# Adding layer 3 into a residual that is already stored: a four-layer network on one core

## The chip, the core and the metric

The kernel runs on one core of a Trainium2 chip. A core has a matrix engine (TensorE, PE in the profile; its weight loads are shown as PEld), a vector engine (VectorE, DVE), a scalar engine (ScalarE, ACT), a general engine (GpSimd, POOL) and a queue engine (SyncE, SP) that here only issues DMAs. Sixteen DMA engines move data between the large memory (HBM) and the on-chip memory (SBUF); PE writes its results into a small accumulation memory (PSUM) from which ACT and DVE take them. Each engine works through its own instruction list in order and waits on semaphores. The metric is the device time of one execution in microseconds, lower is better.

## What is computed

The input x has 16 images of 64 x 64 positions ("tokens", 4096 for each image) with 256 channels. Four layers follow one another, each with the same frame: normalise by groups of channels (`_gn`), compute something, add it to x.

```python
x = x + _L0_conv_ref(_gn(x), L0_conv_embeddings)   # nearest of 1024 code vectors
x = x + _L1_conv_ref(_gn(x), ...)                  # sigmoid attention along image rows
x = x + _L2_conv_ref(_gn(x), ...)                  # gate * _gn(x), gate from an n x n softmax
x = x + _L3_conv_ref(_gn(x), ...)                  # linear attention, output projection, layer norm
return x
```

Of layer 3 the end matters here:

```python
out = jnp.einsum('bhde,bhdn->bhen', context, q)
...
out = jnp.einsum('bxyh,hc->bxyc', out, w_out) + b_out
mu = jnp.mean(out, axis=-1, keepdims=True)
var = jnp.mean(jnp.square(out - mu), axis=-1, keepdims=True)
out = (out - mu) * jax.lax.rsqrt(var + LN_EPS) * gamma + beta
```

All arithmetic is in float32.

## The kernel before

**Stages.** Each image goes through a sequence of Python generators: `stats0` (statistics of x), `stage1` (layer 0, the search for the nearest code), `layer1`, `rows2` and `stage2` (layer 2's exponentials), `gate2` (applies the gate), `stage3` (layer 3). The main loop at the end of the function gives each generator a start time and a length in units of one image's period, puts them in a heap, and always advances the generator whose next step is due first. So the instruction lists of all engines interleave the stages of up to five images, and the order is fixed when the program is built; `LAG` and `LEN` constants set the shifts. In the steady state a period is some 340 us long. Toward the end there are fewer images left to interleave; the last image's layer 3 runs nearly alone.

**Chunks.** An image is worked on in 8 chunks (`NCHUNK`) of 512 tokens (`CW`). Most tiles hold a chunk as 128 partitions by 2 halves (`NK`) of the channels by 512 tokens, that is, channels on the partitions, 512 KB. Chunks go from one stage to the next through HBM: `dram.tile` gives such an array, with a few buffers for each name.

**gate2** (from line 663) loads a chunk of layer 2's input, multiplies it by the gate so that it becomes the input of layer 3, takes statistics (`chunk_stats`), and stores it into the HBM tile `d` (line 691, SP's queue; the profile names it `x_g<-xg_g`). It leaves off an amount that is constant for each channel: `xm_` (line 670), beta minus the mean of layer 2's normalisation, is handed on to `stage3` to be added there.

**stage3, first part** (lines 740 to 796) loads each chunk of that array (line 742, `xk_s<-x_g`), and makes keys, queries and values and the context matrix. The tile `qv` has tag `u4`, two buffers. In its first chunk it also makes `x_row` (line 771): `put_row` turns `xm_` into a row in three bf16 parts, with eight filler matmuls (`busy`, line 133) before it. Queries are stored to HBM and fetched again in the second part (`fetch`, `qo_s<-qd_s`).

**stage3, second part** (lines 797 to 908) is what the change touches. `form`, `variance` and `deviate` run one or two chunks ahead and scale the queries by the layer norm's factor; `variance` ends in a power on GpSimd (line 850). For each chunk the loop at line 872 loads the residual again (line 874, `xo_s<-x_g`), and forms each output bank `px` in PSUM, twice per chunk, from three products: the residual transposed to tokens on partitions (line 884, eight 128 x 128 transposes per chunk), the scaled queries times `wctx` (line 890), and ones times `x_row` (line 894). ACT copies the bank into `y` (line 895), which has tokens on its partitions and tag `u4` too. SP stores y one chunk later (line 905; the last at 908) in the order of the output, rows of 1 KB.

**GpSimd's list.** GpSimd's own DMAs are those of the search: for each tile of 128 tokens an indirect DMA gathers the code vectors from HBM and adds them to the tokens `xc` in SBUF (line 399). Between them stand small operations of all stages: the powers of lines 280 and 850, the queries' maximum and sum (784 and 738). Tokens with codes added are transposed by PE two tiles into the next chunk (`back`, line 362). The input of a chunk of tokens, and all other large loads, are on SP's queue.

## Time and profile before

Three runs took 5756.55, 5736.58 and 5745.39 us, median 5745.39. The profile is of one execution with its own span.

| | us | share of the span |
|---|---|---|
| span, first to last instruction | 5743.5 | |
| out phases of the last four images (first to last eviction of y) | 63, 59, 40, 36 | |
| search's last gather issued at | 5057.6 | |
| TensorE clock granted, mean | | 0.953 of full |
| DMA traffic, mean | | 184 GB/s |

The rest of the profile's lines stand in the prediction. How to read them: "busy" is the time in which an engine executes instructions (several matmuls that overlap count once), "idle before" is the time that the engine stood still just before such an instruction, and what ended that time is its releaser. The chain of waits goes back from the last instruction, at each step to what released it. A row of groups names line, engine, operation, tile written from tiles read, and shape.

### The profile page before, as it was taken

The page shows a single profiled execution, that of the slowest core. Times are in us where ns is not written, and L with a number is a line of the kernel's source. Part 1 is how long each engine was busy: PE and PEld are TensorE (multiplying, and loading weights), DVE is VectorE, ACT ScalarE, POOL GpSimd, SP SyncE. Part 2 cuts the span into 40 slices and gives each one's busy share as a digit, 9 for nine tenths or more (in the row PEclk, how much of TensorE's full clock was granted, in tenths as well). Part 3 has the DMA queues.
Part 4 walks back from the last instruction along what each step waited for, and adds up shares of the span by engine and source line. Part 5 has one row for each costly group of instructions (what it writes and reads, how often), then busy time and mean ns, then how long its engine had stood idle before and what let it go on. Part 6 is the DMA issues. An engine that isn't in the chain of part 4 may idle for free.

```text
span 5743.5 us, 80122 instructions
## 1 busy us (share of the span) xinstructions
PE 5264.6 (92%) x28975; PEld 3227.5 (56%) x28975; DVE 5074.3 (88%) x7186; ACT 4498.8 (78%) x6514; POOL 1721.5 (30%) x1074
## 2 busy tenths in 40 slices
PE   8978899889999999999999999999999999997888
PEld 3534455545656556565655656565565655664556
DVE  6489799999989999998999999999999999998882
ACT  4478588878878788887978788787888879887873
POOL 3123233223333232322323232332323233311221
PEclk9988999989999999999999999999999999998888
DMA  6453836655665656566475656746566674745543
GB/s 184 133 165 93 263 111 196 198 156 170 212 192 174 228 157 217 168 201 223 149 248 158 216 181 198 233 149 223 174 210 194 188 229 151 227 157 180 198 159 116
DMA packets 521380, 1059.52 MB, mean 184 GB/s; under 512 B 52504, under 2 KB 266392, under 8 KB 512792
## 3 DMA queue, kind: packets, MB, share of 16 engines
q1 hardware_dynamic: 406288, 885.11, 45.5%
q0 software_dynamic: 73728, 67.14, 8.2%
q10 hardware_dynamic: 40968, 102.13, 4.6%
q8 instruction: 230, 3.77, 0.3%
q14 instruction: 166, 1.36, 0.1%
HBM read 751.18 MB, written 303.04 MB: 184 GB/s over the span
## 4 chain that ended last, share of the span: by engine, by line
PE 40%; DVE 16%; ACT 11%; issue 4%; DMA 4%; POOL 4%; SPq 0%; ACTq 0%; POOLq 0%; DVEq 0%
PE pd_s L387 12%; DVE ex_s L630 6%; ACT ex_s L627 5%; PE ph_l L477 3%; PE pxo_s L890 3%; PE pqv_s L764 2%; PE pk_s L747 2%; PE po_l L515 2%; DMA qo_s<-qd_s 2%; PE pxo_s L884 2%; PE pz_s L839 2%; POOL qv_s L784 2%; DVE i_s L398 2%; DVE nn_s L393 1%; PE pvr_s L847 1%
## 5 line engine op out<-in xcount | busy, mean ns | idle before, releaser
L630 DVE CUSTOM_DVE_ANT_0 ex_s<-ex_s,x2b 128x2048 f32<-128x2048 f32 x1024 | 2398.0, 2349 | 65.9 <-ACT ex_s L627 65.8
L627 ACT ACTIVATE ex_s<-x0b,nmax_s,x_r 128x2048 f32<-128x2048 f32 x1024 | 2138.1, 2089 | 42.9 <-DVE num_s L630 34.3
L387 PE MATMUL pd_s<-e,xn_s 128*128 128x512 f32 x4096 | 1989.0, 620 | 44.9 <-DVE m L393 33.6
L399 POOL DMA_INDIRECT xc_s<-in_emb_rows,i_s x512 | 1091.3, 2131 | 1926.7 <-DVE i_s L398 1406.6
L387 PEld LDWEIGHTS pd_s<-e,xn_s 128*128 128x128 f32 x4096 | 752.8, 196 | 810.3 <-issue 697.6
L393 DVE CUSTOM_DVE_ANT_0 nn_s<-pd_s,nn_s 128x1024 f32<-128x1024 f32 x512 | 620.2, 1213 | 157.9 <-PE pd_s L387 87.4
L398 DVE FIND_INDEX8 i_s<-m,nn_s 128x8 uint32<-128x1024 f32 x512 | 623.4, 1218 | 0.0
L382 ACT ACTIVATE nn_s<-ne,nx_s 128x1024 f32<-128x1024 f32 x512 | 582.6, 1144 | 45.2 <-DVE nx_s L353 21.5
L477 PE MATMUL ph_l<-wh_l,xt_l 128*128 128x256 f32 x2048 | 525.5, 393 | 20.8 <-DVE m L393 12.1
L764 PE MATMUL pqv_s<-wqv_s,xk_s 128*128 128x256 f32 x2048 | 488.9, 380 | 0.0
L477 PEld LDWEIGHTS ph_l<-wh_l,xt_l 128*128 128x128 f32 x2048 | 382.3, 194 | 135.9 <-issue 64.1
L764 PEld LDWEIGHTS pqv_s<-wqv_s,xk_s 128*128 128x128 f32 x2048 | 388.8, 191 | 119.9 <-issue 60.2
L784 POOL TENSOR_TENSOR qv_s<-qv_s,qm_s 128x512 f32<-128x512 f32 x128 | 195.3, 1526 | 679.9 <-DVE qm_s L783 492.7
L850 POOL TENSOR_TENSOR lrs_s<-lrs_s,mhalf 128x4 f32<-128x4 f32 x128 | 163.6, 1278 | 678.0 <-ACT lrs_s L849 664.2
L515 PEld LDWEIGHTS po_l<-at_l,h_l 64*128 64x128 f32 x4096 | 260.6, 193 | 61.3 <-issue 29.1
L515 PE MATMUL po_l<-at_l,h_l 64*128 64x64 f32 x4096 | 288.7, 283 | 4.5 <-DVE m L393 2.9
L738 POOL TENSOR_TENSOR qv_s<-qv_s,qd_s 128x512 f32<-128x512 f32 x128 | 203.6, 1590 | 266.5 <-DVE qd_s L737 101.4
L890 PE MATMUL pxo_s<-wctx_s,qo_s 128*128 128x256 f32 x1024 | 272.8, 390 | 0.8 <-DVE qo_s L858 0.8
L895 ACT COPY y_s<-pxo_s 128x512 f32<-128x512 f32 x256 | 149.0, 582 | 153.7 <-PE pxo_s L894 131.7
L747 PE MATMUL pk_s<-xk_s,wk_s 128*128 128x512 f32 x512 | 256.6, 624 | 1.5 <-DMA xk_s<-x_g 1.5
L362 PE MATMUL pt_s<-ident,xc_s 128*128 128x128 f32 x1024 | 161.1, 287 | 101.5 <-DMA xc_s<-in_emb_rows,i_s 71.7
L332 ACT ACTIVATE xn_s<-xt_s,nb_n,s_n 128x512 f32<-128x512 f32 x256 | 200.9, 807 | 50.5 <-PE pd_s L387 28.4
(201 smaller groups left out, 7306.4 us busy)
## 6 DMA issues: line engine op xcount, KB each, us to landing
xs_s<-in_xT SPq DMA_DIRECT2D x128, 512.0 KB
xt_s<-in_xT SPq DMA_DIRECT2D x128, 512.0 KB
xc_s<-in_x SPq DMA_DIRECT2D x128, 512.0 KB
x_s<-xt_s ACTq DMA_DIRECT2D x128, 512.0 KB
xt_l<-x_s SPq DMA_DIRECT2D x128, 512.0 KB
x_l<-xt_l SPq DMA_DIRECT2D x128, 512.0 KB
xr_r<-x_l SPq DMA_DIRECT2D x128, 512.0 KB
xg_g<-x_l SPq DMA_DIRECT2D x128, 512.0 KB
```

The costliest lines, as they stand in the source:

```text
L382: nc.scalar.activation(nn, ne2, AF.Identity, bias=nx2[ch][:, t : t + 1])
L387: nc.tensor.matmul(pd[:, cols], lhsT=xn[ch][:, k, t * P : (t + 1) * P], rhs=e2[:, k, cols], start=(k == 0), stop=(k == NK - 1),)
L393: nc.vector.tensor_tensor_reduce(out=nn, in0=pd, in1=nn, scale=1.0, scalar=-3.0e38, op0=ALU.add, op1=ALU.max, accum_out=m8[:, 0:1],)
L398: nc.vector.max_index(i8, m8, nn)
L399: nc.gpsimd.indirect_dma_start(out=xc[ch][:, t, :], out_offset=None, in_=emb_rows, in_offset=bass.IndirectOffsetOnAxis(ap=i8[:, 0:1], axis=0),
L477: nc.tensor.matmul(ph[:, t, :], lhsT=X[:, k, t * P : (t + 1) * P], rhs=wh_n[:, k, :], start=(t % 2 == 0 and k == 0), stop=False, skip_grou ...
L515: nc.tensor.matmul(po[:, r, k * CH + t, :], lhsT=h[rows, t, k * P : (k + 1) * P], rhs=at[rows, t, :], start=True, stop=True,)
L627: nc.scalar.activation(ex, x0b, AF.Exp, bias=nmax[:, T : T + 1], scale=x01[:, T, 1:2], accum_out=den[:, h, T : T + 1])
L630: nc.vector.tensor_tensor_reduce(out=ex, in0=ex, in1=x2b, scale=1.0, scalar=0.0, op0=ALU.mult, op1=ALU.add, accum_out=num[:, h, T : T + 1],)
L747: nc.tensor.matmul(pk, lhsT=wk_n[:, k, :], rhs=xt[:, k, :], start=(k == 0), stop=(k == NK - 1))
L764: nc.tensor.matmul(pqv[:, j, :], lhsT=xt[:, k, t * P : (t + 1) * P], rhs=wqv_n[:, k, :], start=(j == 0 and k == 0), stop=False, skip_group ...
L890: nc.tensor.matmul(px[:, j, :], lhsT=qT[:, t * P : (t + 1) * P], rhs=wctx[:, 1, :], start=False, stop=False, skip_group_check=True,)
```

## The change

`gate2` stores the layer's input into the output array itself, and `stage3` computes only what layer 3 adds, with channels on the partitions, and has it added there by a DMA. Part by part:

- The HBM tile for the gated chunk is gone. `gate2` stores into `out[b]`, whose shape becomes 8 chunks x 128 partitions x 1024 (2 halves x 512 tokens), 4 KB in one run for each partition; the host puts the result back in the order of tokens afterwards. `stage3` loads its first part's chunks from there.
- `x_row`, `by_identity` and the eight fillers are gone. `xm_` is added when y is evicted: `nc.scalar.copy` becomes an activation (Identity) with `xm_` as a bias for each partition.
- The second load of the residual and its transposes are gone. The product with `wctx` is turned round: `wctx` is the stationary operand, one 128 x 128 block for each half of the channels, and the 512 scaled queries stream past it; two such matmuls for each chunk in place of four over 256 columns and two over the row.
- y has channels on its partitions, and is written to `out` by a DMA on GpSimd's queue with `accum_op=ALU.add`, in the same chunk, issued after `variance(ch + 2)`; SP's stores of y are gone.
- `qv` and `y`, which share tag `u4`, ask for three buffers in place of two (4 KB per partition each). SBUF set aside for the rings of descriptors of GpSimd's DMAs shrinks from 16384 bytes (the default) to 4096 bytes per partition.

```diff
--- before.py
+++ after.py
@@ -135,7 +135,7 @@
                 skip_group_check=True,
             )
 
-    h_row, qv_row, x_row = row_tile("h_row"), row_tile("qv_row"), row_tile("x_row")
+    h_row, qv_row = row_tile("h_row"), row_tile("qv_row")
 
     def twice(row):
         return row.unsqueeze(1).to_broadcast([P, 2, C])
@@ -168,13 +168,6 @@
                     skip_group_check=True,
                 )
         return make
-
-    def by_identity(out, v3, plus):
-        for k in range(NK):
-            nc.tensor.matmul(
-                out[:, k * P : (k + 1) * P], lhsT=v3[:, k, :], rhs=ident, start=(k == 0), stop=(k == NK - 1),
-                skip_group_check=True,
-            )
 
 
     e_raw = s2p.tile([P, NK, CODES], F32, tag="x0b", name="e_raw", bufs=2)
@@ -658,7 +651,7 @@
             yield from rest
 
 
-    x3_d, norm3 = {}, {}
+    norm3 = {}
 
     def gate2(b):
         tag = f"g2_{b}"
@@ -668,7 +661,7 @@
 
         xm_ = small.tile([P, NK], F32, tag="xm", name=f"xm_{tag}")
         nc.gpsimd.tensor_tensor(xm_, bet, nmean, ALU.subtract)
-        x3 = []
+        dst = out[b].rearrange("c p (k n) -> c p k n", k=NK)
 
         for ch in range(NCHUNK):
             xt = xg.tile([P, NK, CW], F32, tag="xg", name=f"xg_{tag}_{ch}")
@@ -687,19 +680,16 @@
                 )
             chunk_stats(st3, xt, ch)
             yield 4
-            d = dram.tile([P, NK, CW], F32, tag=f"x3_{ch}", name=f"x3_{tag}_{ch}", bufs=3)
-            nc.sync.dma_start(out=d, in_=xt)
-            x3.append(d)
+            nc.sync.dma_start(out=dst[ch], in_=xt)
         with tc.high_priority(offset=URGENT):
             scale, nmean, _ = gn_finish(st3, "n3", b)
-        x3_d[b], norm3[b] = x3, (scale, nmean, xm_)
+        norm3[b] = scale, nmean, xm_
         yield 2
 
 
     def stage3(b):
         tag = f"s3_{b}"
-        dst = out[b].rearrange("(t p) c -> p t c", p=P)
-        x3 = x3_d.pop(b)
+        x3 = out[b].rearrange("c p (k n) -> c p k n", k=NK)
         scale, nmean, xm_ = norm3.pop(b)
         wk_n = wts.tile([P, NK, P], F32, tag="wk_n", name=f"wk_{tag}")
         nc.sync.dma_start(out=wk_n, in_=w_src[:, :, 1, :])
@@ -754,7 +744,7 @@
                 nc.scalar.activation(al[:, ch : ch + 1], last, AF.Exp, scale=-1.0, bias=now)
             kx = s3p.tile([P, CW], F32, tag="v2", name=f"kx_{tag}_{ch}", bufs=7)
             nc.scalar.activation(kx, pk, AF.Exp, bias=now, accum_out=ks[:, ch : ch + 1])
-            qv = s3p.tile([P, CH, 2, P], F32, tag="u4", name=f"qv_{tag}_{ch}")
+            qv = s3p.tile([P, CH, 2, P], F32, tag="u4", name=f"qv_{tag}_{ch}", bufs=3)
             qvs[ch] = qv
             for pr in range(CH // 2):
                 pqv = bank(f"pqv_{tag}_{ch}_{pr}").rearrange("p (j n) -> p j n", j=2)
@@ -767,8 +757,6 @@
                         )
                 nc.tensor.matmul(pqv, lhsT=ones3, rhs=twice(qv_row), start=False, stop=True, skip_group_check=True)
                 nc.scalar.copy(qv[:, 2 * pr : 2 * pr + 2, :, :].rearrange("p j s n -> p j (s n)"), pqv)
-            if ch == 0:
-                put_row(x_row, xm_, by_identity, f"x_{tag}", idle=8)
             yield 5
             pkt = bank(f"pkt_{tag}_{ch}")
             for t in range(CH):
@@ -868,31 +856,15 @@
         deviate(0)
         variance(1)
         yield 2
-        before = None
         for ch in range(NCHUNK):
-            xt = xb.tile([P, NK, CW], F32, tag="xb", name=f"xo_{tag}_{ch}")
-            nc.sync.dma_start(out=xt, in_=x3[ch])
             qT = qs[ch]
-            y = s3p.tile([P, CH, C], F32, tag="u4", name=f"y_{tag}_{ch}")
-            for pr in range(2):
+            y = s3p.tile([P, NK, CW], F32, tag="u4", name=f"y_{tag}_{ch}", bufs=3)
+            for pr in range(NK):
                 if pr == 1 and ch + 1 < NCHUNK:
                     deviate(ch + 1)
-                px = bank(f"pxo_{tag}_{ch}_{pr}").rearrange("p (j c) -> p j c", c=C)
-                for j in range(2):
-                    t = 2 * pr + j
-                    for k in range(NK):
-                        nc.tensor.matmul(
-                            px[:, j, k * P : (k + 1) * P], lhsT=xt[:, k, t * P : (t + 1) * P], rhs=ident,
-                            is_transpose=True, start=(j == 0 and k == 0), stop=False, skip_group_check=True,
-                        )
-                for j in range(2):
-                    t = 2 * pr + j
-                    nc.tensor.matmul(
-                        px[:, j, :], lhsT=qT[:, t * P : (t + 1) * P], rhs=wctx[:, 1, :], start=False, stop=False,
-                        skip_group_check=True,
-                    )
-                nc.tensor.matmul(px, lhsT=ones3, rhs=twice(x_row), start=False, stop=True, skip_group_check=True)
-                nc.scalar.copy(y[:, 2 * pr : 2 * pr + 2, :], px)
+                px = bank(f"pxo_{tag}_{ch}_{pr}")
+                nc.tensor.matmul(px, lhsT=wctx[:, 1, pr * P : (pr + 1) * P], rhs=qT, start=True, stop=True)
+                nc.scalar.activation(y[:, pr, :], px, AF.Identity, bias=xm_[:, pr : pr + 1])
                 if pr == 0:
                     if ch + 2 < NCHUNK:
                         form(ch + 2)
@@ -901,11 +873,8 @@
                 else:
                     if ch + 2 < NCHUNK:
                         variance(ch + 2)
-                    if before is not None:
-                        nc.sync.dma_start(out=dst[:, (ch - 1) * CH : ch * CH, :], in_=before)
+                    nc.gpsimd.dma_start(out=x3[ch], in_=y, accum_op=ALU.add)
                 yield 3
-            before = y
-        nc.sync.dma_start(out=dst[:, TOK // P - CH :, :], in_=before)
 
 
 
@@ -967,14 +936,15 @@
         ("w_qkv", L3_conv_w_qkv), ("w_out", L3_conv_w_out), ("b_out", L3_conv_b_out),
         ("gamma", L3_conv_gamma), ("beta", L3_conv_beta),
     ]
-    nc = bacc.Bacc("TRN2", target_bir_lowering=False, num_devices=1)
+    nc = bacc.Bacc("TRN2", target_bir_lowering=False, num_devices=1, dynamic_dma_scratch_size=4096)
     arrays, args = {}, []
     for name, a in given:
         a = np.ascontiguousarray(a)
         arrays[f"in_{name}"] = a
         args.append(nc.dram_tensor(f"in_{name}", a.shape, mybir.dt.from_np(a.dtype), kind="ExternalInput").ap())
-    o = nc.dram_tensor("out_0", (x.shape[0], TOK, C), F32, kind="ExternalOutput").ap()
+    o = nc.dram_tensor("out_0", (x.shape[0], NCHUNK, P, NK * CW), F32, kind="ExternalOutput").ap()
     with tile.TileContext(nc) as tc:
         tile_net_kernel(tc, *args, o)
     r = run_bass_kernel_spmd(nc, [arrays], core_ids=[0])
-    return r.results[0]["out_0"].reshape(x.shape)
+    y = r.results[0]["out_0"].reshape(x.shape[0], NCHUNK, P, NK, CW)
+    return y.transpose(0, 1, 4, 3, 2).reshape(x.shape)
```

## The prediction

> **What bounds the kernel now.** I read the busy shares first, then the chain that ended last, then busy time by stretch, then what VectorE (DVE) waits for.
>
> ```profile
> span 5743.5 us, 80122 instructions
> PE 5264.6 (92%) x28975; PEld 3227.5 (56%) x28975; DVE 5074.3 (88%) x7186; ACT 4498.8 (78%) x6514; POOL 1721.5 (30%) x1074
> ...
> q1 hardware_dynamic: 406288, 885.11, 45.5%
> q0 software_dynamic: 73728, 67.14, 8.2%
> ...
> PE 40%; DVE 16%; ACT 11%; issue 4%; DMA 4%; POOL 4%; SPq 0%; ACTq 0%; POOLq 0%; DVEq 0%
> ```
>
> TensorE (PE) is at 92%, VectorE close behind; PE has the largest share of the chain. GpSimd (POOL) is idle for 70%. The next view splits the span into stretches: the first two are the same part of a batch period in different batches, 2874 to 2969 is one steady period's last part of layer 3 (the eight chunks that form y; "out phase" below), the last two are the out phases of the last two batches, where little else runs. Columns: length, busy PE, PEld, DVE, ACT, POOL, then granted clock, DMA share, GB/s.
>
> ```profile
> 1600.00:1851.00 251.00, 235.26 (x1197) 137.72 (x1196) 229.53 (x330) 205.43 (x300) 86.62 (x50) 0.94 0.55 171
> 2634.00:2874.00 240.00, 223.40 (x1204) 132.17 (x1203) 226.02 (x324) 204.89 (x300) 80.95 (x50) 0.99 0.57 179
> 2874.00:2969.00 95.00, 92.72 (x603) 62.88 (x601) 89.47 (x120) 74.41 (x107) 25.48 (x16) 1.00 0.76 242
> 5559.00:5599.00 40.00, 36.54 (x221) 28.52 (x219) 30.29 (x40) 24.62 (x39) 9.04 (x6) 0.99 0.74 248
> 5703.00:5743.00 40.00, 35.63 (x223) 28.86 (x221) 7.83 (x12) 10.97 (x22) 6.04 (x6) 1.00 0.58 185
> ```
>
> In a steady out phase PE is busy 92.7 of 95 us, but DVE is busy 89.5: PE is the first limit and DVE stands 3 us behind it. In the last out phase PE alone is full. The first two rows show how PE work turns into time: at clock 0.94 instead of 0.99 PE is busy 12 us longer, and the stretch is 11 us longer.
>
> **What is removed from PE.** These are the rows of groups, busy time in all and mean of one:
>
> ```profile
> L884 PE MATMUL pxo_s<-ident,xo_s 128*128 128x128 f32 x1024 | 166.5, 284 | 0.0
> L894 PE MATMUL pxo_s<-x_row,ones 128*128 128x512 bf16 x256 | 98.3, 384 | 0.0
> L133 PE MATMUL prow_x_s<-ones 128*128 128x512 bf16 x128 | 30.2, 379 | 0.0
> L174 PE MATMUL prow_x_s<-ident,v_x_s 128*3 128x128 f32 x64 | 10.0, 281 | 4.3 <-ACT v_x_s L146 4.3
> L155 PE MATMUL prow_x_s<-top_x_s,below 3*3 3x256 bf16 x32 | 8.7, 272 | 3.4 <-ACT top_x_s L154 3.4
> ```
>
> The transposes of the residual (L884), the row products (L894) and the whole making of x_row (fillers L133, L174, L155) go: 166.5 + 98.3 + 30.2 + 10.0 + 8.7 = 313.7 us of PE busy time, 19.6 us for each of 16 batches. The product with wctx stays, turned round: before 512 instructions over 256 columns (L890, 1024 records, 272.8 us), after 256 over 512 columns. The nearest row of that shape, L747, has 512 records in 256.6 us, and 512 records are what the new form gives. So 0 to -16 us; I take 0.
>
> **How much of that reaches the end: the steady part, 1500 to 5059 us.** It holds 10.4 periods of about 340 us. Two ceilings: PE loses 19.6 x 10.4 = 204 us there, and VectorE has only 3559.0 - 3314.7 = 244 us idle. What DVE waited for in this stretch (us in total, times, longest):
>
> ```profile
> DVE ex_s L630 <- ACT ex_s L627: 54.3, 48, 2.9
> DVE nn_s L393 <- ACT nn_s L382: 33.6, 31, 3.9
> DVE qz_s L841 <- PE pz_s L839: 19.4, 17, 4.2
> DVE nkm_s L750 <- PE pk_s L747: 17.7, 26, 1.9
> ```
>
> All lines of this view that name PE add up to 89 us, those that name ACT to 129. I take it that with PE 6% lighter the waits on PE go and those on ACT stay: **-89 us**, 8.6 per period. Bounds: 0 (DVE finds another wait) and -134, the chain's pieces in this stretch on L884 (73), L894 (32) and x_row's matmuls (29).
>
> **The clock's share.** Lighter PE work has a price: the first two stretches above show the clock lower and the period 11 us longer where PE pauses more often. Bounds per period: 0 and +11. I take 2, near the clean end, because the work leaves the out phase, the densest one (clock 1.00): **+22 us** over 10.4 periods. The Trainium skill ("TensorE: Matmul & The Clock Gate", What's actually happening) says that the clock falls to half after one idle window of some 3.4 us; by that rule, which speaks against thinning PE, one such window more in each period would be an estimated 1.7 us of lost matmul time, so about +18 us, which agrees with what I took and proves it no more than the rows do.
>
> **Head and tail.** Before 1500 us there is one out phase: -8, as for one period. In the tail the last two out phases take 40 us for eight chunks, about 5.2 us per chunk in the timeline. Per chunk two halves lose 0.46 (L884) + 0.22 (L894) us of chain each, 1.36 us; but the accumulating transfer then wants 3.7 us per chunk (below) and qo's load, 262 KB at 0.047, 0.8, so I take 4.2 instead of 5.2: -8 us each, **-16**. In the two out phases before these, the chain has 16.5 us on L884 and L894 and DVE is busy beside them; half, **-8**.
>
> **The accumulating DMA.** One per chunk, 128 in all, 512 KB each, from GpSimd's queue. No such DMA is in the trace; the nearest is L399, the codebook gather, which adds into its target as well:
>
> ```profile
> L399 POOL DMA_INDIRECT xc_s<-in_emb_rows,i_s x512: 1533/1602/3897, 42.3 to 5057.6; - x171
> ...
> DMA to landing us min/median/max: 3.6/5.6/12.2
> ```
>
> Issuing costs GpSimd 1.6 to 3.9 us; at L399's mean of 2.13 us it is 273 us more on an engine that is idle for 4022. DMA time: the queue table gives q0 8.2% of 16 x 5743.5 us for 67.14 MB, 0.112 us per KB, and q1 0.047. Bounds for 524 KB on 16 engines: 1.6 us as a plain copy, 3.7 us at the gather's rate; I take 3.7, since that row adds too. Removed are the reload of the residual and the plain store of y, 67 MB each at 0.047: 396 us of all 16 engines, against 470 added; the DMA share rises by some 1%, hidden at shares of 0.6 to 0.76.
>
> Order on GpSimd: the new DMA stands behind the power of chunk ch+2 (L850), which waits for an ACT instruction issued after y's eviction, so y is ready when GpSimd gets there. Its other waits (gate store landed, xk read) ended tens of us before. Behind it wait the next gather and the next L850. A gather may thus leave 2.1 us later and queue up to 3.7 behind on the same DMA queue. The fourth gather of a chunk issued at 2894.92 is read by the transposes (L362) from 2910.78, the one at 2944.02 from 2958.29: with 5.6 us to land, 10.3 and 8.7 us of cover against 5.8. So 0; without cover it would be up to 5.8 us at each of some 30 chunk ends, +174.
>
> The Trainium skill speaks against this queue: "SBUF — State Buffer", SBUF: two separate sides, says that GpSimd cannot write descriptors while DVE holds a shared port in some modes. L399's spread, 1.6 to 3.9, agrees that something holds it at times; by the rule each issue could be late by one long DVE instruction, an estimated 2.3 us more, 8.1 against the 8.7 of cover: the sum stays.
>
> Buffers: y shares tag u4 with qv. Three instead of two let y wait for its landing over three chunks: in the tail 12.6 us, against 2.7 (second half and its eviction) + 1.0 (L850) + 5.6 + 2.8 (landing, larger transfer) = 12.1. Tight, but it holds; if not, ACT stands at the eviction and all later ACT work with it. The smaller descriptor ring makes room for this buffer; with landings of 8 us and issues 4 us apart two or three DMAs are open at a time, and I take no wait for the ring: 0.
>
> End: the last plain store is issued at 5739.3 and the span ends 4.2 us later; the new one takes 5.6 + 2.8: **+4**. ACT's eviction changes from a copy (582 ns) to one with a bias (L579, same shape, 683): 256 x 0.10 = +27 us, less 20 for x_row's three ACT groups, beside an ACT that idles 22%: 0. SP loses 128 loads and its 128 waits for y; gate's store and xk's load stay, on another array: 0, at best a few us.
>
> Sum: -89 + 22 - 8 - 16 - 8 + 4 = -95, so a span of 5648; the median of the runs shown is 1.9 us above the profiled span: **5650 us**.
>
> **Rivals.** (1) *The clock takes it all*: every period pays the whole 11 us, 114 in place of 22: -3, 5742 us. For it: PE's clock in the head is 0.88 to 0.96 wherever PE is below 90%. Against: the out phase has it at 1.00. (2) *PE was the only limit*: the chain's pieces vanish whole, 134 + 8 + 39 (tail) - 4 = 177: 5568 us. For it: the 11 us for 12 of the two stretches. Against: DVE's 89.5 of 95. (3) *Slower: the accumulating transfer is slow.* Place: the tail's out phases, where chunks take 4.6 to 8 us and y's buffers hang on it. If one takes T, the last four out phases last 32 T instead of 63 + 59 + 40 + 36 = 198 us; outside them the gain is 89 + 8 - 22 - 4 = 71, so it decides from T = (198 + 71)/32 = 8.4 us, 2.3 times the gather's rate. At T = 11.9, one steady chunk, the loss is 32 x 11.9 - 198 - 71 = 112: 5857 us; beyond that the steady part slows too. Against it: the gather's rate; for it: no row shows an addition into HBM, and HBM must be read and written. (4) *It doesn't do what it says*: a wait between store, load and addition on the one output array, wider than its chunk, would hold SP; its price is rival 3's, and I count it there.
>
> **How the numbers follow.** Forecast 0.53, own range 5595 to 5715 (steady term between 45 and 134, tail 0 to 32). Rival 1: 0.12. Rival 2: 0.13. Rivals 3 and 4: 0.22. The range goes from just below rival 2, 5550, to 5800 (T near 10), which leaves out under 2 in 10. A change under 0.3%, 17 us, can't be told from none here: faster 0.66, same 0.12, slower 0.22.
>
> **What would show it.** After: PE busy near 4950 us and near 86 to 88% of the span; DVE above 89%; steady out phases of 90 to 92 us with PE near 77; the clock no lower than 0.94; one new POOL DMA line x128 of about 2 us, landing within 9 us; y's ACT row without waits on a DMA; last two out phases near 32 us. A landing over 12 us, ACT waiting for y's buffer, or SP waiting for that DMA would make it wrong on the slow side; a DVE share under 88% with waits on ACT or POOL would say that PE was not what DVE waited for.

## The result, and the profile after

The changed kernel took 5767.53 us (median of 5 runs, 5758.93 to 5774.41) against 5745.39 for the kernel before: ratio 1.0041, 95% interval 1.0021 to 1.0061. It is slightly slower, by 22 us, where 95 us less were forecast; the time lies inside the range, on the wrong side of the start. The profiled execution has a span of 5757.2 us. First the page of the changed kernel: busy shares, the two large DMA queues, the chain that ended last.

```profile
span 5757.2 us, 75894 instructions
PE 5151.4 (89%) x26959; PEld 3026.3 (53%) x26959; DVE 5053.7 (88%) x7186; ACT 4509.0 (78%) x6450; POOL 1880.5 (33%) x1201
...
q1 hardware_dynamic: 320272, 750.88, 39.1%
q0 software_dynamic: 92160, 134.26, 15.3%
...
PE 31%; DVE 21%; ACT 12%; issue 7%; DMA 4%; POOL 4%; ACTq 0%; SPq 0%; POOLq 0%; DVEq 0%
```

The work did leave: 2016 matmul records fewer, the transposes and row products among them. But PE's busy time fell by 113 us (5264.6 to 5151.4), not by the 314 that these rows had held. Rows of groups overlap: those of all PE groups add up to 5924 us before and 5702 after. PE lost 9 points of the chain and DVE won 5. By stretches (length; busy PE, PEld, DVE, ACT, POOL; granted clock, DMA share, GB/s): the rest of a steady period, its out phase, and the last out phases of the last two batches:

```profile
2609.00:2856.00 247.00, 226.59 (x1175) 133.20 (x1174) 223.16 (x326) 204.50 (x297) 84.29 (x53) 0.96 0.57 172
2856.00:2950.00 94.00, 88.20 (x513) 51.95 (x513) 90.22 (x120) 76.30 (x107) 33.71 (x22) 0.96 0.77 206
5583.00:5622.00 39.00, 29.92 (x120) 16.11 (x118) 27.73 (x38) 23.96 (x37) 13.99 (x13) 0.95 0.73 137
5717.00:5757.00 40.00, 27.72 (x118) 15.09 (x116) 8.90 (x13) 12.35 (x22) 13.72 (x14) 0.92 0.75 131
```

The thinned out phase is 1 us shorter (94 after 95). PE is busy 88.2 us there instead of the 77 forecast, at a clock of 0.96 instead of 1.00; DVE needs 90.2. The rest of the period, which lost only x_row's making (3 us by its rows), is 247 us instead of 240. So the later batches run at 342 us where they took 337. Ten whole periods, from the first eviction of y in the second batch to that in the twelfth, first in the kernel before, then in the changed one (columns as above):

```profile
1506.00:4888.00 3382.00, 3209.14 (x18088) 1979.22 (x18086) 3147.77 (x4439) 2799.03 (x4056) 1078.85 (x660) 0.98 0.62 195
1501.00:4912.00 3411.00, 3161.64 (x16841) 1866.63 (x16840) 3131.08 (x4444) 2806.83 (x4018) 1202.71 (x740) 0.95 0.62 181
```

The ten periods took 29 us more, with 47 us less of TensorE and as much of VectorE and ScalarE as before, within 17 us. The last stretch, which nothing but this chain fills, has PE busy 8 us less and is 40 us as before: its chunks are 3 us faster together, the landing at the end is 4 us longer. The groups of the new output path (busy, mean ns | idle before, releaser):

```profile
L838 POOL TENSOR_TENSOR lrs_s<-lrs_s,mhalf 128x4 f32<-128x4 f32 x128 | 195.1, 1524 | 154.4 <-ACT lrs_s L837 146.9 <-issue 7.3
L876 POOL DMA_DIRECT2D out<-y_s x128 | 122.0, 953 | 452.0 <-ACT lrs_s L837 224.2 <-ACT y_s L867 219.6 <-issue 3.5
L867 ACT ACTIVATE y_s<-pxo_s,xm_g 128x512 f32<-128x512 f32 x256 | 174.6, 683 | 108.6 <-PE pxo_s L866 105.7 <-issue 1.3 <-ACT xt_s L358 1.2
```

The adding DMA (L876) is cheap to issue, 0.95 us against the 2.13 assumed, and y's eviction (L867) waits for no DMA, so three buffers suffice. Its landing, in the view of this line:

```profile
DMA to landing us min/median/max: 5.4/6.5/8.5
```

That is inside the 9 us asked for. What DVE, and then PE, waited for in 1500 to 5059 us (total, times, longest):

```profile
DVE ex_s L623 <- ACT ex_s L620: 72.8, 38, 3.9
DVE qd_s L726 <- ACT qv_s L773: 46.2, 12, 6.5
DVE qz_s L829 <- PE pz_s L827: 33.5, 24, 5.2
DVE nn_s L386 <- ACT nn_s L375: 25.9, 23, 3.9
DVE nn_s L386 <- PE pd_s L380: 25.6, 22, 2.1
DVE nkm_s L740 <- PE pk_s L737: 19.7, 26, 1.8
```

```profile
PE ph_l L470 <- DVE xt_l L513: 40.8, 27, 3.9
PE pd_s L380 <- DVE m L386: 36.2, 30, 2.3
PE px_s L334 <- ACT sq_s L328: 29.3, 32, 2.7
```

This is the turn of the case. All DVE lines that name PE add up to 113 us where 89 were to vanish; those on ACT rose from 129 to 152. And PE, lighter, now waits for DVE: 125 us in this stretch, 38 before.

### The profile page after: what moved, and what is told of

It reads as the page before. It is cut to its first block, busy times and chain, and to the rows that moved or that the text cites. A ratio compares the mean times of both kernels' runs of the same rounds, so it can differ in the third digit from the quotient of the medians.

```text
span 5757.2 us, 75894 instructions
## 1 busy us (share of the span) xinstructions
PE 5151.4 (89%) x26959; PEld 3026.3 (53%) x26959; DVE 5053.7 (88%) x7186; ACT 4509.0 (78%) x6450; POOL 1880.5 (33%) x1201
## 3 DMA queue, kind: packets, MB, share of 16 engines
q0 software_dynamic: 92160, 134.26, 15.3%
## 4 chain that ended last, share of the span: by engine, by line
PE 31%; DVE 21%; ACT 12%; issue 7%; DMA 4%; POOL 4%; ACTq 0%; SPq 0%; POOLq 0%; DVEq 0%
PE pd_s L380 11%; DVE ex_s L623 8%; ACT ex_s L620 5%; PE ph_l L470 3%; DVE i_s L391 3%; PE pxo_s L866 2%; PE pk_s L737 2%; POOL qv_s L772 2%; DVE nn_s L386 2%; PE pqv_s L754 2%; DVE st_s L251 1%; PE po_l L508 1%; ACT nn_s L375 1%; DMA x0b<-rows_r 1%; PE pz_s L827 1%
## 5 line engine op out<-in xcount | busy, mean ns | idle before, releaser
L623 DVE CUSTOM_DVE_ANT_0 ex_s<-ex_s,x2b 128x2048 f32<-128x2048 f32 x1024 | 2372.6, 2322 | 89.1 <-ACT ex_s L620 88.5
L380 PE MATMUL pd_s<-e,xn_s 128*128 128x512 f32 x4096 | 2039.3, 635 | 71.3 <-DVE m L386 63.0
L392 POOL DMA_INDIRECT xc_s<-in_emb_rows,i_s x512 | 1122.0, 2191 | 1900.9 <-DVE i_s L391 1309.6
L380 PEld LDWEIGHTS pd_s<-e,xn_s 128*128 128x128 f32 x4096 | 775.4, 202 | 889.2 <-issue 743.4
L470 PE MATMUL ph_l<-wh_l,xt_l 128*128 128x256 f32 x2048 | 539.9, 401 | 62.0 <-DVE xt_l L513 40.8
L866 PE MATMUL pxo_s<-qo_s,wctx_s 128*128 128x512 f32 x512 | 286.1, 644 | 15.9 <-DVE qo_s L846 14.3
L728 POOL TENSOR_TENSOR qv_s<-qv_s,qd_s 128x512 f32<-128x512 f32 x128 | 177.9, 1390 | 320.7 <-DVE qd_s L727 204.4
L876 POOL DMA_DIRECT2D out<-y_s x128 | 122.0, 953 | 452.0 <-ACT lrs_s L837 224.2
L867 ACT ACTIVATE y_s<-pxo_s,xm_g 128x512 f32<-128x512 f32 x256 | 174.6, 683 | 108.6 <-PE pxo_s L866 105.7
L838 POOL TENSOR_TENSOR lrs_s<-lrs_s,mhalf 128x4 f32<-128x4 f32 x128 | 195.1, 1524 | 154.4 <-ACT lrs_s L837 146.9
```

The costliest lines, as they stand in the source:

```text
L380: nc.tensor.matmul(pd[:, cols], lhsT=xn[ch][:, k, t * P : (t + 1) * P], rhs=e2[:, k, cols], start=(k == 0), stop=(k == NK - 1),)
L392: nc.gpsimd.indirect_dma_start(out=xc[ch][:, t, :], out_offset=None, in_=emb_rows, in_offset=bass.IndirectOffsetOnAxis(ap=i8[:, 0:1], axis=0),
L470: nc.tensor.matmul(ph[:, t, :], lhsT=X[:, k, t * P : (t + 1) * P], rhs=wh_n[:, k, :], start=(t % 2 == 0 and k == 0), stop=False, skip_grou ...
L623: nc.vector.tensor_tensor_reduce(out=ex, in0=ex, in1=x2b, scale=1.0, scalar=0.0, op0=ALU.mult, op1=ALU.add, accum_out=num[:, h, T : T + 1],)
L866: nc.tensor.matmul(px, lhsT=wctx[:, 1, pr * P : (pr + 1) * P], rhs=qT, start=True, stop=True)
```

## The experiments

Each kernel was timed in five rounds beside the kernel before (5738 to 5742 us in these groups). Ratios are to that kernel, with 95% intervals.

**1. Is it the clock?** If PE, thinned, only lost its clock, discarded matmuls that fill the gaps should win time back. One kernel puts them into the out phase, one at the head of layer 3 where x_row's making had stood.

```diff
                 px = bank(f"pxo_{tag}_{ch}_{pr}")
+                busy(px, 3)
```

> The changed kernel with three filler matmuls (128x512 bf16, 0.22 us of chain each, as in x_row's fillers) before each of the 256 output banks of the second part of layer 3; nothing else differs. That puts back some 169 us of PE time where 265 were removed. Clock theory (the thinner PE list lets the granted clock fall more often, 222 us at half clock between 2874 and 5059 us against 58 before the change, and that costs what was saved): clock up from 0.934 to 0.945 or more, time down from 5767 by 10 to 60 us although PE has more to do. GpSimd theory (the accumulating DMA stands in front of the power of line 838 and holds the layer norm's chain): no gain, 5760 to 5800 us. If PE time simply adds: up to 5850.

Measured: 5818.15 us, 1.0129 (1.0103 to 1.0154), 50 us more than the changed kernel, at a granted clock of 0.942. The ranges of the clock theory and of the GpSimd theory are both missed; only the loose bound of adding PE time holds.

```diff
+            if ch == 0:
+                busy(bank(f"pfl_{tag}"), 8)
```

> The changed kernel with the eight filler matmuls put back in the first chunk of layer 3's first part, where the making of x_row had them, 1.8 us of PE chain per image. Clock theory: if the clock is lost there, 5 to 30 us less than 5767 and clock above 0.934; if it is lost in the thinned second part, no change within 10 us. GpSimd theory: no change, or some us more.

Measured: 5762.94 us, 1.0041 (1.0026 to 1.0057): as without. Filling gains nothing on balance. These runs can't tell a lost clock that costs nothing from one whose return is eaten by the fillers' own work.

**2. Is it the place of the DMA on GpSimd?** The addition is issued half a chunk later.

```diff
+                    if before is not None:
+                        nc.gpsimd.dma_start(out=x3[ch - 1], in_=before, accum_op=ALU.add)
...
-                    nc.gpsimd.dma_start(out=x3[ch], in_=y, accum_op=ALU.add)
```

> The changed kernel with each accumulating DMA issued half a chunk later, after the first eviction of the next chunk, so that GpSimd reaches the power of line 838 without waiting for y. GpSimd theory: GpSimd's waits at the DMA (444 us for y and the lrs eviction) shrink, waits of PE at line 845 (22.7 us) return to some 6 us, time falls by 20 to 60 us. Clock theory: within 15 us of 5767, clock still near 0.93.

Measured: 5776.82 us, 1.0058 (1.0037 to 1.0078). No gain, but the waits that were to shrink did not: GpSimd stood 447 us before the DMA's line in the loop (444 in the changed kernel for the same two releasers), PE waited 22.6 us for the power (22.7), and in the timeline of the tail the DMA still comes just before the power. So this run doesn't test the place of the DMA.

**3. The thinner PE alone.** The kernel before without the residual's reload and its transposes (the residual is missing from the output); GpSimd untouched.

```diff
-            xt = xb.tile([P, NK, CW], F32, tag="xb", name=f"xo_{tag}_{ch}")
-            nc.sync.dma_start(out=xt, in_=x3[ch])
...
-                            px[:, j, k * P : (k + 1) * P], lhsT=xt[:, k, t * P : (t + 1) * P], rhs=ident,
```

> The kernel before the change with the residual's second load and its transposes left out, so the output lacks the residual; everything else, x_row and plain stores included, as before. PE loses 166 us of busy time and nothing is put on GpSimd. If PE is what the steady part waits for (the prediction's step): 5745 less 40 to 90 us. Clock theory: the same thinning by itself loses the clock (below 0.95 from 0.953), and the time stays within 20 us of 5745 or rises. GpSimd theory: a gain of 40 us or more, since GpSimd is untouched.

Measured: 5739.18 us, 0.9998 (0.9983 to 1.0014). 166 us of matmuls (by their row) and 67 MB of loads are gone, with nothing put on another engine, and the time stands still. The same view of DVE's waits, 1500 to 5059 us, for this kernel:

```profile
DVE ex_s L630 <- ACT ex_s L627: 80.4, 56, 3.3
DVE qz_s L841 <- PE pz_s L839: 45.7, 31, 4.4
DVE nn_s L393 <- PE pd_s L387: 19.5, 18, 1.8
```

The wait for pz, 19.4 us before, is 45.7: with fewer matmuls DVE waits more for one of them. In the tail, where little else runs, the benefit is there: from the last index search to the end the profiled kernel takes 665 us, 686 before. Ahead of it the same 22 us are lost again. So the mistake lies in what bounds the batch periods.

**4. VectorE lighter.** Half of the bn_stats go, in the changed kernel and in the one before (the second channel block takes the first one's statistics).

```diff
-        for k in range(NK):
-            nc.vector.bn_stats(st[:, k, ch, :], xt[:, k, :])
+        nc.vector.bn_stats(st[:, 0, ch, :], xt[:, 0, :])
```

> The changed kernel with half of VectorE's statistics left out: of each pair of channel blocks only the first gets its bn_stats, and both means and variances are taken from it (so the normalisations use the wrong numbers for the second block). 512 instructions of 0.68 us are gone, some 330 us of VectorE's 5054 us, 22 us a batch. Nothing else is touched. Theory 'balance' (after the change the matmuls wait for VectorE, the clock falls at each of these pauses, and so the removed matmul work came back as pauses and half clock): with a lighter VectorE the pauses go, the removed TensorE work shows at last: 5767 less 120 to 280 us, 5490 to 5650, PE waits on DVE down from 126 to under 60 us in the stretch 1500 to 5059. Theory 'VectorE alone is the bound': 5767 less 250 to 330, 5440 to 5520, and the same fall in the kernel before. Theory 'the clock takes it, whoever waits' (the granted clock is set by how thin the matmuls are, VectorE has nothing to do with it): 5740 to 5790, clock at or under 0.93.

> The same cut of 330 us of VectorE's statistics in the kernel before. Theory 'balance': there the matmuls hardly wait for VectorE in the steady part (38 us in 1500 to 5059 at a clock of 0.98), TensorE is the longer one, so only the early batches and the ends gain: 5742 less 20 to 110 us, 5630 to 5720, a smaller fall than in the changed kernel by 80 us or more. Theory 'VectorE alone is the bound': 5742 less 250 to 330, 5410 to 5490. Theory 'the clock takes it': 5720 to 5770.

Measured: 5606.28 us in the changed kernel, 0.9771 (0.9754 to 0.9788), and 5608.60 in the one before, 0.9764 (0.9747 to 0.9781). Both fall, by about 161 and 129 us for 331 of VectorE's (by the rows), and end level. For the changed kernel the theory of balance held the time; for the one before none did, and the difference that it wanted, 80 us or more, is 32. PE's waits on DVE, 125 us in 1500 to 5059, were to fall under 60 and came to 83. VectorE counts in both kernels, and not alone, since under half of the cut shows: in the kernel before DVE's waits on PE grow from 89 to 172 us in that stretch. With VectorE lighter, more of its time goes to waiting for TensorE.

**5. TensorE heavier in the kernel before.** The fillers of the first experiment.

```diff
+                pf = bank(f"pxo_{tag}_{ch}_{pr}")
+                busy(pf, 3)
```

> The kernel before with three discarded 512-column matmuls ahead of each output bank of the out phase (768 in all, 169 us of TensorE): the same fillers that cost the changed kernel 50 us. Theory 'balance': the kernel before stands at the knee, TensorE sets the pace of its later batches, so here they cost more than there: 5742 plus 90 to 169, 5830 to 5911. If only a third shows, 5790 as in the changed kernel, TensorE is no more the bound before than after. Theory 'the clock takes it': fillers raise the clock and cost at most 30 us: 5742 to 5772.

Measured: 5774.57 us, 1.0056 (1.0041 to 1.0070): 36 us for 169, and the granted clock rises to 0.964, the highest of all these kernels, while the time rises too. The first two expectations are missed clearly, the third by 3 us, less than the uncertainty: PE is not at a knee in the kernel before, and a fuller clock bought with fillers doesn't pay.

**6. VectorE against TensorE, with large steps.** Every bn_stats issued twice; and a quarter of the search's matmuls left out.

```diff
-        for k in range(NK):
+        for k in (0, 1, 0, 1):
             nc.vector.bn_stats(st[:, k, ch, :], xt[:, k, :])
```

> The kernel before with every bn_stats issued twice into the same slot: 1024 more of 0.68 us on VectorE's queue, 697 us in all, and nothing else changed. Theory 'VectorE paces the kernel before, TensorE follows': a dearer VectorE shows nearly in full, 5742 plus 500 to 700, 6240 to 6440, several times the share that the fillers on TensorE showed (36 of 169 us, a fifth). Theory 'TensorE paces it': VectorE has some 100 to 400 us of room (its idle time), 5742 plus 100 to 350. Theory 'all three engines hold each other, none leads': about half, 5742 plus 300 to 450.

```diff
-                    for k in range(NK):
+                    for k in range(NK - hf):
```

> The kernel before with a quarter of the search's matmuls left out: for the second half of the codes only the first 128 of 256 channels are multiplied, so other codes are chosen. 1024 matmuls of 128x512 fewer, by their row (635 ns of one, 2039 us busy over 4096) 510 us of TensorE. The DMA, VectorE's and ScalarE's work is as before. Theory 'VectorE paces it': 0 to 60 us are gained, 5680 to 5742, with the granted clock lower (0.90 to 0.94). Theory 'TensorE paces it, and the small cut of 166 us was eaten by the clock': a cut three times as large gains 150 us or more, under 5590.

> The same quarter of the search's matmuls left out of the changed kernel: 510 us of TensorE less. Theory 'VectorE paces it': 0 to 60 us gained, 5705 to 5767. Theory 'TensorE still paces it': under 5615.

Measured: VectorE heavier, 6267.41 us, 1.0925 (1.0896 to 1.0954), +527; TensorE lighter in the kernel before, 5714.51, 0.9947 (0.9927 to 0.9967), -26; in the changed kernel 5676.69, 0.9887 (0.9865 to 0.9909), some 90 below it without the cut, which lies between the two expectations. For the kernel before, both ranges of 'VectorE paces' held. The stretch 1500 to 5059 us of the kernel with the heavier VectorE (columns as above):

```profile
1500.00:5059.00 3559.00, 3178.65 (x17218) 1945.58 (x17217) 3378.15 (x4833) 2675.57 (x3842) 1029.19 (x621) 0.93 0.56 176
```

DVE is busy 95% of it, and PE drops to 89% and a clock of 0.93 although not one matmul was removed: here TensorE's share and clock followed VectorE. The same stretch of the kernel before with the lighter TensorE, and what DVE waited for in it:

```profile
1500.00:5059.00 3559.00, 3208.20 (x18297) 2009.79 (x18296) 3283.29 (x4662) 2937.53 (x4263) 1169.49 (x695) 0.94 0.62 195
```

```profile
DVE nn_s L393 <- ACT nn_s L382: 52.7, 32, 4.1
DVE qd_s L736 <- ACT qv_s L785: 50.5, 12, 6.0
...
DVE qz_s L841 <- PE pz_s L839: 19.8, 15, 2.6
DVE ctx_s L791 <- PE pc_s L789: 19.3, 15, 2.1
...
DVE nkm_s L750 <- PE pk_s L747: 16.2, 18, 1.5
```

With 510 us of matmuls gone (by their rows), all DVE lines that name PE still add up to 88 us in this stretch, 89 before the cut. The lines for pz and pk read as before (19.4 and 17.7). So here these waits don't measure how full TensorE is. They are not fixed either: 128 us with the fillers of experiment 5, 35 with the heavier VectorE, and in the changed kernel the cut took them from 113 to 81.

**7. What the adding DMA costs.** The changed kernel with layer 3's part stored plainly, from SyncE and then from GpSimd (the output holds the part without the residual).

```diff
-                    nc.gpsimd.dma_start(out=x3[ch], in_=y, accum_op=ALU.add)
+                    nc.sync.dma_start(out=x3[ch], in_=y)
```

> The changed kernel with layer 3's part stored to the output by SyncE's queue instead of added there by GpSimd's DMA: the output holds the part without the residual. GpSimd loses 122 us of issuing and the power no longer stands behind it. Theory: the 20 to 25 us by which the changed kernel is slower than the lean form of the kernel before (5739) come from that DMA on GpSimd and in the queues: 5735 to 5750. Rival: they come from the other parts (the turned output matmul, ACT's copy with a bias, the third buffer): 5760 to 5775 as the changed kernel.

> The changed kernel with layer 3's part stored (not added) by the same DMA from GpSimd at the same place: the output holds the part without the residual. With SyncE's store the kernel took 5736, with GpSimd's adding DMA 5767. Theory 'the issuing on GpSimd is the cost' (the power stands behind it): 5760 to 5772. Rival 'the adding transfer is the cost' (it reads and writes, lands later, keeps buffers): 5733 to 5745.

Measured: from SyncE 5736.29 us, 0.9998 (0.9987 to 1.0009); from GpSimd 5746.81, 1.0017 (1.0002 to 1.0033); adding, 1.0041. So it is with the adding DMA on GpSimd that the kernel loses, and the rest of the change is worth nothing on balance. How it splits between issuing and adding, 11 and 14 to 21 us, is not much more than the uncertainty; the expectations for the plain store from GpSimd were missed, by 13 us ('the issuing') and by 2 ('the adding transfer'). The plain store from GpSimd, rows as above:

```profile
L838 POOL TENSOR_TENSOR lrs_s<-lrs_s,mhalf 128x4 f32<-128x4 f32 x128 | 169.2, 1322 | 152.3 <-ACT lrs_s L837 143.2 <-issue 7.2
...
L876 POOL DMA_DIRECT2D out<-y_s x128 | 80.9, 632 | 445.8 <-ACT lrs_s L837 224.3 <-ACT y_s L867 213.1 <-issue 3.8
```

Against it the addition makes the power 0.20 and the issue 0.32 us longer, and the landing 6.5 us in place of 3.9. From the last index search to the end the profiled kernels take 659 us with the plain store and 677 with the addition (661 from SyncE), while up to there they are within 5 us: most of the difference lies in the tail, where the power stands on the chain of every chunk. PE waited 22.7 us for the power with the addition, 19.0 with the plain store and 13.0 with SyncE's, 6.4 in the kernel before. That kernel has 686 us in the tail: with SyncE's store the change gains 25 us there, and it loses 19 ahead of it, without any adding DMA.

**8. Can it be turned to use?** First the gate's product of the second channel block, 100 us by its row, is moved from VectorE to GpSimd; then the residual is added by TensorE in the changed layout, with an identity matmul; then both.

```diff
+                v = xt[:, k, :]
+                nc.gpsimd.tensor_tensor(v, v, nmean[:, k : k + 1].to_broadcast([P, CW]), ALU.add)
+                nc.gpsimd.tensor_tensor(v, v, u, ALU.mult)
```

> The kernel before, with the gate's (x + nmean) * u of the second channel block computed by two tensor_tensor of GpSimd instead of VectorE's scalar_tensor_tensor: 128 instructions of 0.81 us, some 100 us, leave VectorE; 256 of about 1.4 us, some 360 us, come to GpSimd, which is busy 30%. Theory 'VectorE paces': by the 0.39 us gained per us removed in the cut statistics 5740 less 40, between 5685 and 5715. Rival 'GpSimd's new work delays the gathers and the softmax, or the statistics behind it wait': 5745 to 5800.

> The same move of 100 us from VectorE to GpSimd in the changed kernel, whose GpSimd also issues the adding DMA (33% busy). Theory 'VectorE paces': 5767 less 40 to 50, 5710 to 5735. Rival 'GpSimd has become the narrow queue': no gain, 5760 to 5820.

```diff
-                nc.tensor.matmul(px, lhsT=wctx[:, 1, pr * P : (pr + 1) * P], rhs=qT, start=True, stop=True)
+                nc.tensor.matmul(px, lhsT=wctx[:, 1, pr * P : (pr + 1) * P], rhs=qT, start=True, stop=False)
+                nc.tensor.matmul(px, lhsT=ident, rhs=xt[:, pr, :], start=False, stop=True)
```

> The changed kernel with the residual added by TensorE: the stored part is loaded again by SyncE's queue, one matmul with the identity (256 of 128x512, by the row's 0.64 us some 130 to 165 us) adds it into the same bank, and SyncE stores the sum; no DMA from GpSimd but the gathers. Theory 'VectorE paces, and the adding DMA is what made the change slower': as with the plain store, 5730 to 5755. Rival 'the thin TensorE is what made it slower or the reload delays': 5760 to 5790.

> Both: the residual added by TensorE and the gate's second block on GpSimd. Theory 'VectorE paces': 5740 less 40 to 50, 5680 to 5710, the lowest of these four or level with e13. Rival: as e13's, 5745 to 5800.

Measured: 5767.72 us, 1.0057 (1.0037 to 1.0077); 5814.42, 1.0126 (1.0095 to 1.0157); 5744.73, 1.0009 (0.9993 to 1.0026); 5773.86, 1.0071 (1.0050 to 1.0093). TensorE's addition gives the loss back, as expected, and no more. The move to GpSimd lost 28 to 47 us in all three, as the rivals had it. Rows of the kernel before with the move:

```profile
L855 POOL TENSOR_TENSOR lrs_s<-lrs_s,mhalf 128x4 f32<-128x4 f32 x128 | 225.1, 1758 | 456.2 <-ACT lrs_s L854 447.8 <-issue 8.4
L692 POOL TENSOR_TENSOR xg_g<-xg_g,u_g 128x512 f32<-128x512 f32 x128 | 211.6, 1653 | 227.1 <-ACT u_g L684 225.6 <-DMA xg_g<-x_l 1.0
L258 DVE BATCH_NORM_STATS2 st_g<-xg_g 128x6 f32<-128x512 f32 x256 | 166.6, 680 | 27.3 <-POOL xg_g L692 27.1
```

DVE now stands 27 us before the statistics, waiting for GpSimd, where it waited 0.1; its busy time fell by 36 us, not 100 (the gate's row fell by 86, but the row of L630 grew by 35); and the power, the same instruction, went from 1.28 to 1.76 us. Work that was gone from VectorE paid in experiment 4; work that VectorE then has to wait for did not pay here. No version here beats the kernel before with all its work done.

## Why the prediction failed

All the slopes in one place; us of engine time changed, by the rows (the fillers by the 0.22 us of chain each that were expected of them; their rows hold 216 to 220), and what the time did:

| engine, kernel | work | time | share |
|---|---|---|---|
| VectorE, before | +662 to 697 | +527 | 0.76 to 0.80 |
| VectorE, before | -331 | -129 | 0.39 |
| VectorE, changed | -331 | -161 | 0.49 |
| TensorE, before | -166 | -1 | 0 |
| TensorE, before | -510 | -26 | 0.05 |
| TensorE, before | +169 | +36 | 0.21 |
| TensorE, changed | -510 | about -90 | 0.18 |
| TensorE, changed | +169 | +50 | 0.30 |

Since rows overlap, the engine's whole busy time moved by less than they say. Measured by that, the shares are 0.84, 0.52 and 0.54 for VectorE, in the table's order, and 0.01, 0.09, 0.30, 0.30 and 0.43 for TensorE: the order of the two engines holds, the gap is smaller. All these slopes belong to the places where the work was changed: the statistics, the search and the out phase.

**The step that failed is the steady term, -89 us**: "I take it that with PE 6% lighter the waits on PE go and those on ACT stay". They did not go (113 us; 116 in experiment 3; 88 in the kernel before with 510 us of matmuls less), and those on ACT rose to 152. The first reading behind it, "PE is the first limit and DVE stands 3 us behind it", took the higher busy share for the limit. At 92% and 88%, both near full, the shares don't rank the engines: PE's busy time contains its own slow clock (the search's matmuls took 620 ns in the mean at a clock of 0.953, 641 at 0.923), and with VectorE heavier it rose by 165 us without a matmul more. Of the two, VectorE sets the pace; its idle 7% in the steady part is made of some 240 waits of 1 us in the mean, the longest 4.8 us, for single products of TensorE, ScalarE and GpSimd, and a lighter TensorE did not remove them. That they are round trips through the engines is argued from their length and number. That they are no backlog of TensorE is shown for the kernel before only (experiment 6). The bound of 0 was named ("DVE finds another wait"), with too little weight; the batches even lost some 20 us.

**The removed work, 313.7 us**, was too large a ceiling. It adds up rows that overlap with others: with these 1504 instructions taken out of the trace of the kernel before, and all else left in its place, PE is busy 5121.5 us, 143 less. And rows that stayed grew, the search's from 1989.0 to 2039.3 us. The product turned round, put at 0 to 16 us less, holds 286.1 us where it held 272.8. So PE near 4950 us was not to be had.

**The clock term, +22** (twice 10.4 is 21), had the right sign: the clock fell, from 0.953 to 0.934 over the span. The reading behind it is not in its rows: the stretch at clock 0.94 is not one "where PE pauses more often", since PE is idle 15.7 us in it and 16.6 in the stretch at 0.99. What the periods did shows better in several kernels. Here are the ten periods of each, cut at the first and the last eviction of y, in us for one period:

| kernel | out phase | rest | period | clock in the rest |
|---|---|---|---|---|
| before | 96.3 | 242.0 | 338.3 | 0.974 |
| before, lean (experiment 3) | 94.2 | 246.0 | 340.2 | 0.965 |
| changed | 93.5 | 247.6 | 341.1 | 0.946 |
| changed, SyncE's store (7) | 93.5 | 247.8 | 341.2 | 0.943 |
| changed, residual by TensorE (8) | 100.0 | 238.1 | 338.0 | 0.963 |
| before, fillers (5) | 104.7 | 237.3 | 342.0 | 0.982 |
| before, VectorE heavier (6) | 115.1 | 258.9 | 374.0 | 0.927 |

Where the out phase gets shorter, the rest gets longer, and the other way round: in the first six rows, in which TensorE's work in the out phase differs, the period stays within 4 us. It grows by 36 when VectorE's work does. The thinner kernels lose 2 to 3 us per period. The lower clock goes along with that, but it doesn't set the rest alone: at 0.965 and 0.963 the rest takes 246 and 238 us. No run changes the clock and nothing else, so what a lost clock costs here stays open. Rival 1, "the clock takes it all", had the nearest time of the four, 5742; it too had the waits on PE vanish, so its nearness is luck in part. The Trainium skill ("TensorE: Matmul & The Clock Gate", What's actually happening), weighed in the prediction, has the direction as the traces show it (0.953, lean 0.944, changed 0.934); that section doesn't say what such a window costs a kernel in which another engine leads.

**The adding DMA.** Priced at 3.7 us of 16 engines; the queue table gives (15.3 - 8.2)% of 5757.2 over 128, 3.2 us. Rival 3, the slow transfer (from 8.4 us for each), is excluded by these 3.2 us and by a median landing of 6.5 (the longest is 8.5). The other rule weighed, of a shared port ("SBUF — State Buffer", SBUF: two separate sides), with an estimated 2.3 us more per issue, does not show at the issue of this DMA, whose longest is 1.57 us where 2.13 was the mean assumed; whether it delays landings, no run here tells. The step "the new DMA stands behind the power of chunk ch+2" was wrong: the order put it in front, as the waits of GpSimd in the changed kernel show, where it holds the queue for y:

```profile
POOL out L876 <- ACT lrs_s L837: 224.2, 51, 10.0
POOL out L876 <- ACT y_s L867: 219.6, 53, 10.1
```

What that order costs is not shown, since experiment 2 left it as it was. "So 0" for GpSimd was wrong by 25 to 31 us (with the adding DMA against SyncE's store, by ratios and by medians). The rows speak for a longer power and the issue in front of it, and against late gathers, whose cover held (PE waited 71.0 us for them, 71.7 before).

**Head and tail.** -8, -16, -8, +4 were forecast for out phases and end. The last four out phases came to 62, 50, 39 and 33 us against 63, 59, 40 and 36, so 14 less where 24 were taken; with SyncE's plain store they came to 60, 44, 34 and 30, 29 less. The first out phase took 80 us for 88, the 8 less that were forecast, and from the last eviction to the end it is 7.9 us in place of 4.2, as taken. From the last index search on, the kernel is 9 us shorter. So the thinner chain gave the tail at least what was forecast, and the adding DMA took a good half of it back. Buffers, ACT's dearer eviction and SyncE at nothing: these held as far as the rows show.

**What stays open.** Why the thinner kernels lose 2 to 3 us in each period ahead of the tail. Why the cut of 510 us gave 90 us in the changed kernel and 26 in the one before. What the order of instructions does apart from the amount of work: the first five full periods became 1 to 6 us shorter with the change, the later ones some 5 longer. And ScalarE, busy 78% and waited for by VectorE longer than TensorE (129 us against 89 in the steady part before), was never made lighter or heavier, so its share in the pace is untested. The split of the profiled kernels into periods and tail rests on one execution of each.

## What to carry to other kernels

When two engines are both near 90% busy, don't take the fuller one for the limit: find the slope, by adding and removing work on each, before an edit is priced; in the kernel before, statistics added on VectorE cost three quarters of their time, matmuls taken off TensorE gave next to nothing. Don't add up rows of groups that overlap and call it the engine's saving. A wait of the leading engine on another does not mean that the other one is too busy: ask whether it is a backlog or a round trip. And a free engine is only free if no one on the path waits for it.

## What the runs showed of the hardware

A DMA from GpSimd that adds 512 KB into HBM took 0.93 us to issue and 6.5 us to land (medians), a plain store in its place 0.61 and 3.9. It counted 3.2 us of all 16 engines, the plain one (11.2 - 8.2)% of 5735.9 over 128, 1.3. GpSimd's power of 128x4 took 1.28 us in the mean in the kernel before, 1.33 in the changed one with SyncE's store, 1.32 beside the plain store from GpSimd, 1.52 beside the adding one and 1.76 beside 256 more tensor instructions of its own engine. The search's matmuls took 620 ns in the mean at a granted clock of 0.953, 635 at 0.934 and 641 at 0.923. And matmul rows of 314 us, removed, lowered TensorE's busy time by 113, since they overlapped with others and the rows that stayed grew.
